# A new split of products between VectorE and GpSimd, and an input load whose last columns come in sixteen small pieces

## The chip, the core and the metric

The kernel runs on one core of one Trainium2 chip. The metric is the device time of one execution in microseconds (us), shorter is better. A profile gives the span from the first to the last instruction, and beside it the time of the very execution that was profiled.

## What is computed

For each of 4096 rows of 256 float32 numbers, all products of two of its numbers, i and j with j not below i, in the order of the upper triangle:

```python
def _L0_rec_ref(inputs):          # inputs: (4096, 256) float32
    d = inputs.shape[1]
    dot = jnp.einsum('bi,bj->bij', inputs, inputs)
    iu, ju = jnp.triu_indices(d)
    return dot[:, iu, ju]         # (4096, 32896) float32
```

The input has 4.2 MB, the output 4096 x 32896 x 4 bytes, 539 MB.

## The kernel before, in words

**Tiles and stages.** Each of the 128 partitions holds 32 rows of the input, and the whole input stays in SBUF as the tile `xt` (8192 numbers per partition, 512 of them for each pair of rows). Work goes two input rows at a time (`REPEAT`). The 32896 output columns of such a pair are cut into three pieces (`PIECES`): piece 0 has columns 0 to 10943, piece 1 columns 10944 to 21887, piece 2 the last 11008. Sixteen pairs of three pieces make 48 pieces. A piece is computed into one of two places in SBUF (`places`, the tiles o0 and o1, `o` in the profile) and then stored by a DMA of SP's queue. While one place is being stored, the other is filled. A place may be filled again when the store from it has landed (the semaphores `free`).

**A row of products.** "Row" in the code is a run of output columns with the same i: the products of number i with the numbers from i upwards, up to 256 long for i = 0 and 1 long for i = 255. Piece 0 holds 47 such rows (256 down to 203 long), piece 1 63 rows (the first of them a rest of 7 columns, then 209 down to 18 of the last one), piece 2 148 rows (147 down to 1). `vector_ops` puts two neighbouring rows into one instruction of double length where it can; what juts out of the first of them is overwritten later, and `interleave` and `schedule` lay the instructions out so that an overwriting one waits only for work that is long done. One instruction covers both input rows, so its number of elements per partition is twice the columns: 128x2x512 is a pair of rows 256 long for two input rows.

**The engines.** VectorE (`vector`) multiplies with one operand from SBUF (`xv`, a copy of the current pair's input) and one from PSUM (`xp`, another copy). GpSimd (`gpsimd`) reads both operands from `xv`. In the first two pieces (`AHEAD`), ScalarE helps (`scalar`). From then on a loop runs: its body covers six pieces (`PASS`) and is run eight times on VectorE and GpSimd, each by its own branch; the last two pieces of a body belong to the next pass and stand in an `If`.

**What sets the order.** The order is written out by hand. In the loop `blocks` cuts the rows of a piece at index `k = share(block)`: before the change the first k rows (the long ones) are VectorE's and the rest GpSimd's. `share` takes the k at which the larger of two estimates is least, `vector_time` of the first part and `gpsimd_time` of the second plus `LATER`. GpSimd starts a piece when VectorE's first instruction of it is done (semaphore `go`); VectorE's last instruction of a piece waits for GpSimd's last (`g_done`). SP waits for `v_done` and issues the store.

**The loads.** SP issues all input loads at the start, ahead of the first store on the same queue: the first pair of rows (128x512, semaphore `loaded[0]`) and all others (128x7680, `loaded[1]`). VectorE and GpSimd wait for the second one before the loop only.

Of the kernel before, what the change touches and what calls it, by code (L numbers as in the profile page):

```python
# [12 lines left out]
P = 128  # L13
UNIT = 64
REPEAT = 2
# [7 lines left out]
AHEAD = 2  # L23


LATER = 1.0
FIRST = [3968]
DIRECT = 1
COPY = 700
# [7 lines left out]
def runs(d: int, lo: int, hi: int) -> list:  # L37


    found, at = [], 0  # L40
    for i in range(d):
        a, b = max(at, lo), min(at + d - i, hi)
        if a < b:
            found.append((i, i + a - at, a, b - a))
        at += d - i
    return found


def vector_ops(block: list) -> list:

    ops, k = [], 0
    while k < len(block):
        i, j, at, n = block[k]
        m = 2 if k + 2 < len(block) and i == j else 1
        ops.append((block[k], m))
        k += m
    return ops  # L60
# [32 lines left out]


def vector_time(block: list) -> float:
    return sum(68 + 1.046 * REPEAT * n * m for (*_, n), m in vector_ops(block))


def gpsimd_time(block: list) -> float:
    return sum(142 + 1.66 * REPEAT * n * m for (*_, n), m in vector_ops(block))  # L100
# [6 lines left out]
def split(block: list, alone: bool, busy: list) -> int:  # L107

    def ends(k: int) -> list:
        vector = sum(vector_time([run]) for run in block[k:]) if alone else vector_time(block[k:])  # L110
        return [busy[0] + scalar_time(block[:k]), busy[1] + vector]

    k = min(range(len(block) + 1), key=lambda k: max(ends(k)))
    busy[:] = ends(k)
    return k


def tail(block: list, budget: float) -> int:
    return next(k for k in range(len(block)) if gpsimd_time(block[k:]) <= budget * 1e3)


def share(block: list) -> int:
    return min(range(len(block)), key=lambda k: max(vector_time(block[:k]), gpsimd_time(block[k:]) + LATER * 1e3))


def window(ap: bass.AP, free: list) -> bass.AP:
# [4 lines left out]
def kernel(  # L131
# [15 lines left out]
    nc = tc.nc  # L147
    n, d = x.shape
    width = out.shape[1]
    each, groups = REPEAT * d, n // (P * REPEAT)  # L150
# [8 lines left out]
    x_in = x.rearrange("(p g) d -> p (g d)", p=P)  # L159
# [5 lines left out]
    xt = pool.tile([P, groups * each], F32, name="x")  # L165
# [5 lines left out]
    def semaphore(name: str):  # L171
        return ctx.enter_context(nc.semaphore(name))

    free = [semaphore(f"free{k}") for k in range(PLACES)]
    head, v_done, a_done, go = (semaphore(s) for s in ("head", "v_done", "a_done", "go"))
    loaded = [semaphore(f"loaded{k}") for k in range(2)]

    def take(engine, sem, value: int):
        engine.wait_ge(sem, value).then_inc(sem, -value)  # L179
# [7 lines left out]
    def blocks(p: int, ahead: bool):  # L187

        lo, hi = spans[p % PIECES]
        alone = ahead and p == 0  # L190
        cuts, busy = [lo, *(FIRST if alone else []), hi], [0, 0]
        for c, (a, b) in enumerate(zip(cuts, cuts[1:])):
            block = runs(d, a, b)
            if c == DIRECT:
                busy[1] += COPY
            if ahead:
                if p == HELPED:
                    block = block[: tail(block, HELP)]
                k = split(block, alone, busy)
                yield a - lo, b - lo, block[:k], block[k:], lo  # L200
            else:
                k = share(block)
                yield a - lo, b - lo, block[k:], block[:k], lo

# [9 lines left out]
    def vector(h, pieces: range, ahead: bool, done: int = 0, joined: int = 0) -> tuple:  # L216
        for p in pieces:
            place, copied = places[p % PLACES], None
            parts = blocks(p, ahead)
            if ahead and p == 0:  # L220
                for c, (_, _, _, block, lo) in enumerate(parts):
# [67 lines left out]
    def scalar(pieces: range):  # L289

        xa = xt[:, :each]
        for p in pieces:
            for _, _, block, _, lo in blocks(p, True):
                todo = [
                    nc.scalar.activation(  # L295
                        places[p][:, r, at - lo : at - lo + length],
                        xa[:, r * d + j : r * d + j + length],
                        AF.Copy,
                        scale=xa[:, r * d + i : r * d + i + 1],
                    )  # L300
                    for i, j, at, length in block
                    for r in range(REPEAT)
                ]
                if todo:
                    todo[-1].then_inc(a_done, 1)
                else:
                    nc.scalar.sem_inc(a_done, 1)

    def gpsimd(h, pieces: range, ahead: bool, done: int = 0, turns: int = 0) -> tuple:
# [6 lines left out]
        for p in [HELPED] if ahead else pieces:  # L316
            place = places[p % PLACES]
            block, lo = helped(p) if ahead else next((block, lo) for _, _, block, _, lo in blocks(p, False))
            turns += not ahead
            order = interleave(block)  # L320
            waits = schedule(order)
            counted = {*waits.values()}
            number = {k: done + 1 + c for c, k in enumerate(sorted(counted))}
            for k, ((i, j, at, length), m, _) in enumerate(order):
                at -= lo
                ins = nc.gpsimd.tensor_tensor(  # L326
                    place[:, :, at : at + m * length],
                    window(xv[:, j:], [[d, REPEAT], [1, m], [1, length]]),
                    window(xv[:, i:], [[d, REPEAT], [1, m], [0, length]]),
                    ALU.mult,  # L330
                )
                if k == 0 and not ahead:
                    ins._wait_ge(go, turns)
                elif k in waits:
                    ins._wait_ge(g_own, number[waits[k]])
                if k in counted:
                    ins.then_inc(g_own, 1)
            done += len(counted)
            ins.then_inc(g_done, 1)
        return done, turns  # L340

    def sync():
        done = ahead_done = 0
        for turn in range(passes * PASS):
            h, p = divmod(turn, PASS)
            ahead, place = turn < AHEAD, places[p % PLACES]
            parts = list(blocks(p, ahead))
            for lo, hi, *_, base in parts:
                done += 1
                if ahead:  # L350
                    ahead_done += 1
                    nc.sync.wait_ge(a_done, ahead_done)
                to = x_out[h, p // PIECES, :, :, base + lo : base + hi]
                store = nc.sync.dma_start(to, place[:, :, lo:hi])
                store._wait_ge(v_done, done)
                store.then_inc(free[p % PLACES] if len(parts) == 1 else head, 16)
        for sem, count in ((v_done, done), (a_done, ahead_done)):
            nc.sync.sem_inc(sem, -count)

    def settle(engine, counts: tuple):  # L360
        for sem, count in zip((v_own, g_done) if engine is nc.vector else (g_own, go), counts):
            if count:
                engine.sem_inc(sem, -count)  # L363

    def all_pieces(engine, pieces_of):
        settle(engine, pieces_of(0, range(AHEAD), True))
        for sem in loaded[1:]:
            engine.wait_ge(sem, 16)
        kind = engine.engine
        with nc.Fori(  # L370
            0,
            passes,
            engines=OrderedEngineSet([kind]),
            head_slot={kind: 0},
        ) as h:
            counts = pieces_of(h, range(AHEAD, PASS), False)
            with engine.If(h < passes - 1):
                nxt = nc.s_assert_within(h + 1, 0, passes - 1)
                settle(engine, pieces_of(nxt, range(AHEAD), False, *counts))
        if engine is nc.vector:  # L380
            nc.vector.wait_ge(v_own, counts[0]).then_inc(v_done, 1)
        settle(engine, counts)

    for (lo, hi), sem in zip(((0, each), (each, groups * each)), loaded):
        nc.sync.dma_start(xt[:, lo:hi], x_in[:, lo:hi]).then_inc(sem, 16)
    nc.vector.memset(edge, 0.0).then_inc(warm, 1)  # L386
    take(nc.scalar, warm, 1)
    nc.scalar.activation(edge[:, :1], edge[:, 1:2], AF.Copy, scale=edge[:, 2:3])  # L388
# [5 lines left out]
    for engine, pieces_of in ((nc.vector, vector), (nc.gpsimd, gpsimd)):  # L394
        all_pieces(engine, pieces_of)
    sync()
    for sem in loaded:
        take(nc.sync, sem, 16)
    for k in range(PLACES):
        take(nc.sync, free[k], 16 * uses)  # L400

# [26 lines left out]
```

## Time and profile before

| what | value |
|---|---|
| median of 3 runs | 1264.88 us (1264.6 to 1265.08) |
| the profiled execution's own time | 1265.03 us |
| its span | 1262.8 us |
| VectorE (DVE) busy | 821.9 us, 65% |
| GpSimd (POOL) busy | 751.5 us, 60% |
| ScalarE (ACT) busy | 27.1 us, 2% |
| DMA | 543.22 MB, mean 430 GB/s |

The profiled execution lies inside the range of the runs, 0.15 us above their median; 2.2 us of it lie outside the span. Busy shares are means over the span; the DMA rate is that of all 16 DMA engines of the core together.

### The profile page before, as it was taken

The page shows a single profiled execution, that of the slowest core. Times are in us where ns is not written, and L with a number is a line of the kernel's source. Part 1 is how long each engine was busy: PE and PEld are TensorE (multiplying, and loading weights), DVE is VectorE, ACT ScalarE, POOL GpSimd, SP SyncE. Part 2 cuts the span into 40 slices and gives each one's busy share as a digit, 9 for nine tenths or more (in the row PEclk, how much of TensorE's full clock was granted, in tenths as well). Part 3 has the DMA queues.
Part 4 walks back from the last instruction along what each step waited for, and adds up shares of the span by engine and source line. Part 5 has one row for each costly group of instructions (what it writes and reads, how often), then busy time and mean ns, then how long its engine had stood idle before and what let it go on. Part 6 is the DMA issues. An engine that isn't in the chain of part 4 may idle for free. (4 is left out here: it accounts for less than half of the span.)

```text
span 1262.8 us, 2727 instructions
## 1 busy us (share of the span) xinstructions
DVE 821.9 (65%) x1234; ACT 27.1 (2%) x72; POOL 751.5 (60%) x1131
## 2 busy tenths in 40 slices
DVE  7657766677566775766657666576656766567660
ACT  8000000000000000000000000000000000000000
POOL 5556755567556664666546665576645766467650
DMA  9999999999999999999999999999999999999997
GB/s 390 433 442 426 441 426 438 430 437 434 433 436 432 434 433 434 432 436 431 436 430 440 427 441 426 441 425 442 427 440 427 439 428 438 428 441 428 439 433 331
DMA packets 13623, 543.22 MB, mean 430 GB/s; under 512 B 816, under 2 KB 816, under 8 KB 944
## 3 DMA queue, kind: packets, MB, share of 16 engines
q1 hardware_dynamic: 13616, 543.17, 99.5%
q14 instruction: 7, 0.06, 0.0%
HBM read 4.19 MB, written 538.97 MB: 430 GB/s over the span
## 5 line engine op out<-in xcount | busy, mean ns | idle before, releaser
L267 DVE TENSOR_TENSOR o<-xv,xp 128x504 f32<-128x504 f32 (+59 forms) x1175 | 791.1, 745 | 402.1 <-DMA out_dram<-o 264.2
L326 POOL TENSOR_TENSOR o<-xv 128x64 f32<-128x64 f32 (+61 forms) x1125 | 750.7, 708 | 466.1 <-DVE o L267 465.8
L295 ACT ACTIVATE o<-x 128x256 f32<-128x256 f32 (+34 forms) x70 | 25.5, 457 | 1.0 <-DMA x<-in_r_inputs_dram 1.0
L246 DVE COPY xp<-x 128x512 f32 x15 | 10.3, 686 | 0.0
L228 DVE TENSOR_TENSOR o<-x,xp 128x454 f32<-128x454 f32 (+17 forms) x18 | 9.4, 599 | 0.0
L228 DVE TENSOR_TENSOR o<-x 128x498 f32<-128x498 f32 (+8 forms) x9 | 5.3, 658 | 2.7 <-DMA x<-in_r_inputs_dram 2.7
L244 DVE COPY xv<-x 128x512 f32 x15 | 6.4, 426 | 0.6
L312 POOL MEMSET xv<- 128x1 f32 x1 | 0.1, 98 | 10.1 <-POOLq L179 10.1
L388 ACT ACT_TABLE_LOAD x1 | 1.3, 1283 | 1.2 <-ACTq L179 1.2
L386 DVE MEMSET edge<- 128x32 f32 x1 | 0.1, 85 | 1.0 <-SPq L169 1.0
L223 DVE COPY xp<-x 128x512 f32<-128x512 f32 x1 | 0.7, 681 | 0.0
L313 POOL COPY xv<-x 128x512 f32<-128x512 f32 x1 | 0.6, 609 | 0.0
L388 ACT ACTIVATE edge<-edge 128x1 f32<-128x1 f32 x1 | 0.3, 294 | 0.0
L415 POOL MEMSET const-float32-0.0<- 128x1 f32 x1 | 0.1, 98 | 0.2 <-issue 0.2
L415 POOL MEMSET const-bfloat16-1.0<- 128x1 bf16 x1 | 0.1, 101 | 0.0
L415 POOL MEMSET const-uint8-127<- 128x1 uint8 x1 | 0.1, 101 | 0.0
L415 POOL MEMSET const-float32-1.0<- 128x1 f32 x1 | 0.1, 98 | 0.0
## 6 DMA issues: line engine op xcount, KB each, us to landing
out_dram<-o SPq DMA_DIRECT2D x31, 10944.0 KB, 35.1
out_dram<-o SPq DMA_DIRECT2D x16, 11008.0 KB, 32.9
out_dram<-o SPq DMA_DIRECT2D x1, 6976.0 KB, 21.4
out_dram<-o SPq DMA_DIRECT2D x1, 3968.0 KB, 13.9
x<-in_r_inputs_dram SPq DMA_DIRECT2D x1, 3840.0 KB, 12.4
x<-in_r_inputs_dram SPq DMA_DIRECT2D x1, 256.0 KB, 2.8
```

The source lines that it names most:

```text
L223: nc.vector.tensor_copy(xp, x_of(h, 0)).then_inc(v_own, 1)
L228: ins = nc.vector.tensor_tensor(place[:, :, at - lo : at - lo + length], window(x_of(h, 0)[:, j:], [[d, REPEAT], [1, 1], [1, length]]), wi ...
L244: ins = nc.vector.tensor_copy(xv[:, :each], x_of(h, p // PIECES))
L246: nc.vector.tensor_copy(xp, x_of(h, p // PIECES)).then_inc(v_own, 1)
L267: ins = nc.vector.tensor_tensor(place[:, :, at : at + m * length], window(xv[:, j:], [[d, REPEAT], [1, m], [1, length]]), window(xp[:, i:] ...
L295: nc.scalar.activation(places[p][:, r, at - lo : at - lo + length], xa[:, r * d + j : r * d + j + length], AF.Copy, scale=xa[:, r * d + i ...
L312: nc.gpsimd.memset(xv[:, each:], 0.0).then_inc(g_own, 1)
L313: nc.gpsimd.tensor_copy(xv[:, :each], x_of(0, 0)).then_inc(g_own, 1)
L326: ins = nc.gpsimd.tensor_tensor(place[:, :, at : at + m * length], window(xv[:, j:], [[d, REPEAT], [1, m], [1, length]]), window(xv[:, i:] ...
L386: nc.vector.memset(edge, 0.0).then_inc(warm, 1)
L388: nc.scalar.activation(edge[:, :1], edge[:, 1:2], AF.Copy, scale=edge[:, 2:3])
L415: nc = _bacc.Bacc("TRN2", target_bir_lowering=False, num_devices=1)
```

## The change

Two edits, independent of one another.

The split in the loop: GpSimd now takes the first rows of a piece, which are the longest, and VectorE all rows after them. `share` takes the smallest k for which the estimate of VectorE's remaining rows is at most `BUDGET`, 19.5 us, and the constants of that estimate are new. The first two pieces are unchanged.

The load of the input: the second load is 64 columns (256 bytes) narrower, and these last 64 columns come in 16 further loads of 1, 2, 3 and so on to 15 rows, and 8 rows, partition after partition, with a semaphore of their own, for which VectorE and GpSimd wait before the loop.

```diff
-LATER = 1.0
+LAST = [k * (k + 1) // 2 for k in range(16)]
+BUDGET = 19.5
...
 def vector_time(block: list) -> float:
-    return sum(68 + 1.046 * REPEAT * n * m for (*_, n), m in vector_ops(block))
+    return sum(122 + 0.979 * REPEAT * n * m for (*_, n), m in vector_ops(block))
...
 def share(block: list) -> int:
-    return min(range(len(block)), key=lambda k: max(vector_time(block[:k]), gpsimd_time(block[k:]) + LATER * 1e3))
+    return next(k for k in range(len(block)) if vector_time(block[k:]) <= BUDGET * 1e3)
...
                 k = share(block)
-                yield a - lo, b - lo, block[k:], block[:k], lo
+                yield a - lo, b - lo, block[:k], block[k:], lo
...
-        for sem in loaded[1:]:
-            engine.wait_ge(sem, 16)
+        engine.wait_ge(loaded[1], 16)
+        engine.wait_ge(loaded[2], 16 * len(LAST))
...
-    for (lo, hi), sem in zip(((0, each), (each, groups * each)), loaded):
-        nc.sync.dma_start(xt[:, lo:hi], x_in[:, lo:hi]).then_inc(sem, 16)
+    def load(rows: slice, lo: int, hi: int, sem):
+        nc.sync.dma_start(xt[rows, lo:hi], x_in[rows, lo:hi]).then_inc(sem, 16)
+
+    load(slice(0, P), 0, each, loaded[0])
+    load(slice(0, P), each, groups * each - UNIT, loaded[1])
+    for k, lo in enumerate(LAST):
+        load(slice(lo, LAST[k + 1] if k + 1 < len(LAST) else P), groups * each - UNIT, groups * each, loaded[2])
```

In the third item that `blocks` yields stand GpSimd's rows, in the fourth VectorE's. The columns and instructions of each piece in the loop, counted from the code:

| piece | VectorE before | VectorE after | GpSimd before | GpSimd after |
|---|---|---|---|---|
| 0 | 7018 columns, 17 instructions | 8676, 22 | 3926, 12 | 2268, 7 |
| 1 | 7074, 22 | 8298, 27 | 3870, 15 | 2646, 10 |
| 2 | 7605, 36 | 6328, 59 | 3403, 44 | 4680, 21 |
| sum | 21697, 75 | 23302, 108 | 11199, 71 | 9594, 38 |

All of GpSimd's (POOL's) instructions of piece 0 in the loop before; in each, 128 partitions, two input rows, and the columns of one or two rows of products:

```order
L326 TENSOR_TENSOR o_60<-xv 128x2x454
L326 TENSOR_TENSOR o_60<-xv 128x2x448
L326 TENSOR_TENSOR o_60<-xv 128x2x442
L326 TENSOR_TENSOR o_60<-xv 128x2x432
L326 TENSOR_TENSOR o_60<-xv 128x2x426
L326 TENSOR_TENSOR o_60<-xv 128x2x225
L326 TENSOR_TENSOR o_60<-xv 128x2x222
L326 TENSOR_TENSOR o_60<-xv 128x2x438
L326 TENSOR_TENSOR o_60<-xv 128x2x214
L326 TENSOR_TENSOR o_60<-xv 128x2x211
L326 TENSOR_TENSOR o_60<-xv 128x2x217
L326 TENSOR_TENSOR o_60<-xv 128x2x203
```

The same place on GpSimd after:

```order
L327 TENSOR_TENSOR o_60<-xv 128x2x256
L327 TENSOR_TENSOR o_60<-xv 128x2x510
L327 TENSOR_TENSOR o_60<-xv 128x2x252
L327 TENSOR_TENSOR o_60<-xv 128x2x502
L327 TENSOR_TENSOR o_60<-xv 128x2x248
L327 TENSOR_TENSOR o_60<-xv 128x2x253
L327 TENSOR_TENSOR o_60<-xv 128x2x249
```

The rows 247 to 256 long have gone to GpSimd, all shorter ones to VectorE; seven instructions stand where twelve stood.

The start of SP's queue, before against after (from the first loads on; the rows go on with the loads of 8, 9 and up to 15 rows, one of 8 rows, and then the stores):

```order
+L386 DMA x<-in_r_inputs_dram 128x512
+L386 DMA x<-in_r_inputs_dram 128x7616
+L386 DMA x<-in_r_inputs_dram 1x64
+L386 DMA x<-in_r_inputs_dram 2x64
+L386 DMA x<-in_r_inputs_dram 3x64
+L386 DMA x<-in_r_inputs_dram 4x64
+L386 DMA x<-in_r_inputs_dram 5x64
+L386 DMA x<-in_r_inputs_dram 6x64
+L386 DMA x<-in_r_inputs_dram 7x64
```

Sixteen DMAs of SP now stand between the second load and the first store, where there were none.

More of the change, by code (lines that the diff above doesn't have):

```diff
@@ L175 @@
     head, v_done, a_done, go = (semaphore(s) for s in ("head", "v_done", "a_done", "go"))
-    loaded = [semaphore(f"loaded{k}") for k in range(2)]
+    loaded = [semaphore(f"loaded{k}") for k in range(3)]
     def take(engine, sem, value: int):
@@ L396 @@
     sync()
-    for sem in loaded:
-        take(nc.sync, sem, 16)
+    for sem, count in zip(loaded, (1, 1, len(LAST))):
+        take(nc.sync, sem, 16 * count)
     for k in range(PLACES):
```

## The prediction

> **What bounds the kernel now.** I read the page's head, queues and issues first, then the rate of the DMA by stretches, then the waits, then one pass of three pieces in the timeline. The page:
>
> ```profile
> span 1262.8 us, 2727 instructions
> ...
> q1 hardware_dynamic: 13616, 543.17, 99.5%
> q14 instruction: 7, 0.06, 0.0%
> ...
> out_dram<-o SPq DMA_DIRECT2D x31, 10944.0 KB, 35.1
> out_dram<-o SPq DMA_DIRECT2D x16, 11008.0 KB, 32.9
> ...
> x<-in_r_inputs_dram SPq DMA_DIRECT2D x1, 3840.0 KB, 12.4
> x<-in_r_inputs_dram SPq DMA_DIRECT2D x1, 256.0 KB, 2.8
> ```
>
> The 16 DMA engines are busy 99.5% of the span with SP's queue. By stretches (after the counts come the clock, the share of the 16 DMA engines, GB/s):
>
> ```profile
> 41.50:1248.00 1206.50, 797.03 (x1191) 0.00 (x0) 734.24 (x1109) 1.00 1.00 434
> ...
> 1249.00:1255.40 6.40, 0.00 (x0) 0.00 (x0) 0.00 (x0) 1.00 0.95 413
> 1255.40:1256.10 0.70, 0.00 (x0) 0.00 (x0) 0.00 (x0) 1.00 0.15 63
> 1256.10:1257.90 1.80, 0.00 (x0) 0.00 (x0) 0.00 (x0) 1.00 0.11 49
> 1257.90:1261.20 3.30, 0.00 (x0) 0.00 (x0) 0.00 (x0) 1.00 0.06 27
> 1261.20:1262.80 1.60, 0.00 (x0) 0.00 (x0) 0.00 (x0) 1.00 0.00 0
> ```
>
> In the loop nothing is left: 434 GB/s at a share of 1.00, 27.1 GB/s per engine. A store of 10944 KB (11.21 MB) takes 25.8 us. The end is what can still move. From 1256.1 on only one or two of the 16 engines work (0.11 x 16 = 1.8), from 1257.9 to 1261.2 exactly one, at its full 27 GB/s. All engines get the same bytes, so one DMA engine has fallen 5.1 us (1261.2 less 1256.1) behind fourteen others over 49 stores, a second one 1.8 us; the end waits for the first. Call it the late engine.
>
> The compute engines, in the waits:
>
> ```profile
> POOL o L326 <- DVE o L267: 465.8, 46, 14.1
> DVE o L267 <- DMA out_dram<-o: 264.2, 31, 9.5
> DVE o L267 <- DVEq L179: 109.3, 14, 9.9
> DVE o L267 <- POOL o L326: 11.9, 15, 0.8
> ```
>
> VectorE waits 264.2 + 109.3 = 373.5 us in 45 pieces, 8.3 us each, for a store that must land first (L179 is the same wait, taken in VectorE's queue); GpSimd waits behind VectorE. Neither sets the end.
>
> **The split, as compute time.** One pass (pieces 2, 0, 1, then 2 again) in the timeline (start, duration, engine, idle before):
>
> ```profile
> 118.75 18.67 DVE L267 TENSOR_TENSOR o<-xv,xp 128x260 f32<-128x260 f32 x36 [9.39 <-DMA out_dram<-o]
> 119.25 17.77 POOL L326 TENSOR_TENSOR o<-xv 128x328 f32<-128x328 f32 x44 [10.93 <-DVE o L267]
> ...
> 144.69 15.41 DVE L267 TENSOR_TENSOR o<-xv,xp 128x1024 f32<-128x1024 f32 x16 [6.21 <-DVEq L179]
> 145.99 14.87 POOL L326 TENSOR_TENSOR o<-xv 128x908 f32<-128x908 f32 x12 [8.96 <-DVE o L267]
> 160.89 0.64 DVE L267 TENSOR_TENSOR o<-xv,xp 128x466 f32<-128x466 f32 x1 [0.79 <-POOL o L326]
> 171.44 16.40 DVE L267 TENSOR_TENSOR o<-xv,xp 128x14 f32<-128x14 f32 x22 [9.91 <-DVEq L179]
> 171.69 15.12 POOL L326 TENSOR_TENSOR o<-xv 128x688 f32<-128x688 f32 x15 [10.84 <-DVE o L267]
> 197.10 13.28 DVE L267 TENSOR_TENSOR o<-xv,xp 128x260 f32<-128x260 f32 x24 [9.26 <-DMA out_dram<-o]
> ```
>
> Single products, by form (mean ns last):
>
> ```profile
> L326 POOL TENSOR_TENSOR o<-xv 128x908 f32<-128x908 f32 x12 | 20.4, 1698 | 108.9 <-DVE o L267 108.9
> ...
> L267 DVE TENSOR_TENSOR o<-xv,xp 128x1024 f32<-128x1024 f32 x12 | 14.7, 1221 | 75.8 <-DVEq L179 38.1 <-DMA out_dram<-o 37.7
> ...
> L326 POOL TENSOR_TENSOR o<-xv 128x320 f32<-128x320 f32 x12 | 8.6, 717 | 0.0
> ...
> L267 DVE TENSOR_TENSOR o<-xv,xp 128x512 f32<-128x512 f32 x12 | 8.1, 677 | 0.0
> ```
>
> VectorE's element costs (1221 - 677)/512 = 1.06 ns, GpSimd's (1698 - 717)/588 = 1.67 ns. Elements are twice the columns in the table of the change. Piece 0: 7018 columns are 14036 elements, 14.9 us; VectorE's 15.41 + 0.64 = 16.05 us leave 1.14 us for 17 products, 0.07 us each. Piece 2 gives 0.07 too, piece 1 0.06. GpSimd: 17.77 us less 6806 x 1.67 ns leaves 6.4 us for 44 products, 0.146 us each. After:
>
> - piece 0: VectorE 17352 x 1.0625 ns + 22 x 0.067 us = 19.9 us (was 16.05, and 0.79 of waiting for GpSimd); GpSimd 4536 x 1.668 ns + 7 x 0.146 us = 8.6 us (was 14.87).
> - piece 1: VectorE 16596 x 1.0625 ns + 27 x 0.062 us = 19.3 us (was 16.40); GpSimd 10.3 us (was 15.12).
> - piece 2: VectorE 12656 x 1.0625 ns + 59 x 0.07 us = 17.6 us; GpSimd 9360 x 1.668 ns + 21 x 0.146 us = 18.7 us, begun 0.5 us later, so that VectorE's last product waits for it: 19.4 us in all (was 18.67).
>
> So stores are issued at most 3.1 us later (piece 0: 19.9 against 16.84). What hides this: a store must start before the one ahead has left the queue. A place's store ends, 1.6 us later it counts as landed (the last row of stretches has 1.6 us without a byte), the piece is computed, and about 1 us after its issue the transfer can start. The store between takes 25.8 us, so a piece may take 23.2 us before the late engine runs dry: 3.3 us to spare at 19.9. The other engines are up to 5.1 us ahead and will run dry late in the run; they wait for the late one anyhow. Compute costs 0. The price from the forms alone, with no overlap of neighbouring products ((677 - 512 x 1.0625) = 133 ns each), would be 21.4 us for piece 0, still inside.
>
> **The split, as seen by the late engine.** No view names what holds this engine up. In the single packets behind the views, which no view groups, its packets are stretched mostly while compute engines run many short products; the other engines' are not. The price is bounded by who gets the blame for 5.1 us. A pass has 75 VectorE and 71 GpSimd products before, 108 and 38 after, 146 both times. All GpSimd's: 5.1 x (38/71 - 1) = -2.4 us. All VectorE's: 5.1 x (108/75 - 1) = +2.2 us. By the count of both, or by neither: 0. I take 85% GpSimd, since the stretched packets cluster in piece 2, where GpSimd has 44 products and VectorE 36, more strongly than the sum of both would have it: -0.85 x 2.4 + 0.15 x 2.2 = -1.7 us. No gain can exceed 3.3 us, since the second engine ends at 1257.9.
>
> The Trainium skill speaks against any effect: its page "SBUF — State Buffer", section "Who interferes with whom", says that a DMA never contends with a compute engine, apart from descriptors that GpSimd writes (here SP issues all). By that rule the split is worth 0 and the sum is the time of before; no run here shows yet which holds.
>
> **The loads.** SP's queue:
>
> ```profile
> L385 SPq DMA_DIRECT2D x<-in_r_inputs_dram x2: 390/403/416, 1.0 to 1.4; - x2
> ...
> DMA to landing us min/median/max: 2.8/7.6/12.4
> ...
> 0.96 0.86 SPq L385 DMA_DIRECT2D x<-in_r_inputs_dram  x2
> 9.58 0.40 SPq L354 DMA_DIRECT2D out_dram<-o  x1
> ...
> 2.00:12.80 10.80, 8.94 (x16) 9.77 (x26) 2.01 (x4) 1.00 1.01 388
> ```
>
> The last row is a stretch again: the first load is issued at 0.96 us and all engines are busy from 2.0 us on, which is the 1 us from issue to start used above.
>
> Sixteen issues more take 16 x 0.403 = 6.4 us: SP is done at 1.82 + 6.4 = 8.3 us, 1.3 us before the first store is issued at 9.58, which waits for products. And the engines have the second load to move until 1.4 + 12.4 = 13.8 us, so a store issued 2 or 3 us late would still lose nothing. If an issue of a short load took over 0.48 us, SP would be late, and from 0.6 us on the queue would run dry.
>
> The bytes are the same. What 16 loads cost the DMA engines before the first store has no row. Lower bound: a gain of 0.1 us, for an engine that gets none of the 128 short rows (2 KB less at 27 GB/s). Upper bound: one after the other, each with the 2.8 us of the first load, 45 us. The nearest row is that of the stores: 35.1 us from issue to landing for 25.8 us of transfer, at a share of 1.00, so the queue works through a later DMA without waiting for the earlier one's landing. I take 0.1 us, and 0 for the end unless the late engine is one that gets many. An offset on any other engine costs nothing below 5.1 us.
>
> The waits for the new semaphore stand before the loop, behind the two first pieces, and so behind loads that the queue carries out before the first store. VectorE's 108 products of code instead of 75 in a pass, is not refetched as long as the loop stays resident: the page has 7 packets of instructions in the whole span, though the body ran eight times.
>
> **The sum.** 1264.88 - 1.7 + 0 = 1263.2 us. The profiled execution (span 1262.8, itself 1265.03, 2.2 us outside the span) lies 0.15 us over the median; the difference of -1.7 is set against the median.
>
> **Rivals.**
>
> - Nothing moves (1264.9). The late engine's stretches go by the number of all products, or have nothing to do with them; this is also the page's rule. For: compute is hidden, the count stays 146. Against: the clustering in piece 2.
> - More is gained (1261.7): GpSimd's products are all of it and the second engine becomes the end, -2.4 to -3.3 us.
> - VectorE's products are the cause: +2.2 us, 1267.1. Against: piece 2 has just twice VectorE's products of piece 0, but almost four times GpSimd's.
> - Slower, by the loads: the short loads run one after the other on one engine, each for its own latency. It decides from 5.1/16 = 0.32 us per load on; at 2.8 us each, less 5.1 us of lead, about +40 us, 1305. Against: the stores' row above.
> - VectorE becomes the bound: from 23.2 us per piece on, each us more costs half a us per piece, some 23 us in 46 pieces. Against: the forms' upper price of 21.4.
>
> **How the numbers follow.** About 0.2%, 2.5 us, is what a measurement of this kernel can tell from no change; faster means below 1262.4, slower above 1267.4. Forecast, around -1.7 (-1.0 to -2.6): 0.45, a quarter of it beyond -2.5. Nothing moves: 0.25. More is gained: 0.15. VectorE the cause: 0.05, a fifth of it beyond +2.5. The loads in series: 0.06. VectorE bound or loop code fetched anew: 0.04. Faster: 0.11 + 0.15 = 0.26, and 0.04 for what an offset of the engines against one another might bring that I can't price, 0.30. Slower: 0.01 + 0.06 + 0.04 = 0.11, of which I keep 0.10. Same: 0.60. The range reaches from the ceiling of the gain, 1261.4, to 1265.8, just above the case in which nothing moves; the forecast's own is 1262.2 to 1263.9.
>
> **What would show it.** After: VectorE's pieces 0 and 1 at 19 to 20 us, its wait for stores down to 5 or 6 us per piece, its wait for GpSimd moved to piece 2; DMA share 1.00 in the loop; the single engine's tail at 27 GB/s shortened from 5.1 to about 3.4 us; the first store issued by 10 us. Wrong: the tail as long as before (nothing moves); a share below 1.00 in the loop (VectorE bound); a first store long after 10 us, or a gap behind the loads; more packets of instructions.

## The result and the profile after

The changed kernel takes 1266.91 us (median of 20 runs, 1266.47 to 1267.22) against 1264.93 us before in the same series: 1.0016 times as long, 95% interval 1.0009 to 1.0023. It is 2.0 us slower, where 1263.2 us and a range up to 1265.8 us were forecast. The profiled execution took 1266.93 us, its span is 1265.1 us (1262.8 before).

The page of the changed kernel: span, GpSimd's and VectorE's busy time, the queue, the large groups, and the DMA issues.

```profile
span 1265.1 us, 2746 instructions
...
DVE 899.3 (71%) x1752; ACT 27.1 (2%) x72; POOL 600.4 (47%) x613
...
q1 hardware_dynamic: 13872, 543.17, 99.5%
q14 instruction: 7, 0.06, 0.0%
...
L268 DVE TENSOR_TENSOR o<-xv,xp 128x156 f32<-128x156 f32 (+4 forms) x1693 | 868.5, 590 | 326.0 <-DMA out_dram<-o 193.5
L327 POOL TENSOR_TENSOR o<-xv 128x476 f32<-128x476 f32 (+20 forms) x607 | 599.5, 1027 | 620.0 <-DVE o L268 619.8
...
out_dram<-o SPq DMA_DIRECT2D x31, 10944.0 KB, 32.3
out_dram<-o SPq DMA_DIRECT2D x16, 11008.0 KB, 31.8
out_dram<-o SPq DMA_DIRECT2D x1, 6976.0 KB, 23.2
out_dram<-o SPq DMA_DIRECT2D x1, 3968.0 KB, 16.1
x<-in_r_inputs_dram SPq DMA_DIRECT2D x1, 3808.0 KB, 13.1
```

The DMA is as full as before (99.5%), and the code is not fetched anew (7 packets). The one row that has grown for the worse is the first store, the 3968 KB one: 16.1 us from issue to landing where it took 13.9. The stores of the loop land sooner after their issue (32.3 against 35.1), since they are issued later.

One pass in the timeline of the changed kernel (start, duration, engine, idle before):

```profile
121.36 17.16 DVE L268 TENSOR_TENSOR o<-xv,xp 128x448 f32<-128x448 f32 x58 [7.39 <-DMA out_dram<-o]
122.06 18.69 POOL L327 TENSOR_TENSOR o<-xv 128x260 f32<-128x260 f32 x21 [15.90 <-DVE o L268]
140.78 0.16 DVE L268 TENSOR_TENSOR o<-xv,xp 128x2 f32<-128x2 f32 x1 [2.27 <-POOL o L327]
...
147.27 19.61 DVE L268 TENSOR_TENSOR o<-xv,xp 128x988 f32<-128x988 f32 x22 [5.05 <-DVEq L180]
148.53 8.62 POOL L327 TENSOR_TENSOR o<-xv 128x512 f32<-128x512 f32 x7 [7.78 <-DVE o L268]
173.23 19.19 DVE L268 TENSOR_TENSOR o<-xv,xp 128x784 f32<-128x784 f32 x27 [6.34 <-DVEq L180]
```

Pieces of 19.6, 19.6 and 19.2 us, and VectorE still waits 5 us and more for a landed store ahead of each. The engines' rates by stretches, the load's end first, then the loop and the end (the last two columns are the share of the 16 DMA engines and GB/s; a packet counts whole in the stretch in which it starts, so a share can come out above 1):

```profile
13.20:16.20 3.00, 3.00 (x7) 3.00 (x9) 3.00 (x3) 1.00 1.06 342
...
41.50:1248.00 1206.50, 874.43 (x1709) 0.00 (x0) 583.09 (x591) 1.00 1.00 433
...
1254.90:1258.30 3.40, 0.00 (x0) 0.00 (x0) 0.00 (x0) 1.00 0.93 401
...
1258.60:1260.20 1.60, 0.00 (x0) 0.00 (x0) 0.00 (x0) 1.00 0.06 28
1260.20:1263.50 3.30, 0.00 (x0) 0.00 (x0) 0.00 (x0) 1.00 0.06 27
1263.50:1265.10 1.60, 0.00 (x0) 0.00 (x0) 0.00 (x0) 1.00 0.00 0
```

The tail of a single engine is still there, until 1263.5 now, 5.1 us after most others (1258.4). What is new stands in the first row. In the same 3 us before the change, the first store moved 434 GB/s:

```profile
13.20:16.20 3.00, 3.00 (x7) 3.00 (x9) 3.00 (x3) 1.00 1.01 434
```

At a share of 1.06 the engines count as busy and move a fifth less. The short loads themselves take little of that: in the single packets, which no view lists, each of the 128 rows of 256 bytes takes 18 ns, between 12.9 and 14.3 us, 2.3 us in all over 16 engines. It is the packets of the first store behind them that are stretched: those of 15872 bytes take 635 ns on average, up to 1791, where they took 592 before. And not on all engines. The packets bear no engine's name, but on one engine a packet starts where the one before it ends, and by that they can be followed, not always surely: an engine that carried 16 short rows loses 1.7 us in the first store, one with 12 about 1.3, one with 9 or 10 about 1.0, one with 5 or fewer nothing.

So the theory (A): the loads cost the time, by holding up the first store on those DMA engines that carry many short rows; the late engine is one of these, so its delay comes out at the end. The rivals: the split costs it (B), or each edit has a half (C).

### The profile page after: what moved, and what is told of

The parts are those of the page before. It is cut to its first block, busy times and chain, and to the rows that moved or that the text cites. A ratio compares the mean times of both kernels' runs of the same rounds, so it can differ in the third digit from the quotient of the medians.

```text
span 1265.1 us, 2746 instructions
## 1 busy us (share of the span) xinstructions
DVE 899.3 (71%) x1752; ACT 27.1 (2%) x72; POOL 600.4 (47%) x613
## 3 DMA queue, kind: packets, MB, share of 16 engines
q1 hardware_dynamic: 13872, 543.17, 99.5%
## 5 line engine op out<-in xcount | busy, mean ns | idle before, releaser
L268 DVE TENSOR_TENSOR o<-xv,xp 128x156 f32<-128x156 f32 (+4 forms) x1693 | 868.5, 590 | 326.0 <-DMA out_dram<-o 193.5
L327 POOL TENSOR_TENSOR o<-xv 128x476 f32<-128x476 f32 (+20 forms) x607 | 599.5, 1027 | 620.0 <-DVE o L268 619.8
L247 DVE COPY xp<-x 128x512 f32 x15 | 10.3, 686 | 0.0
## 6 DMA issues: line engine op xcount, KB each, us to landing
out_dram<-o SPq DMA_DIRECT2D x31, 10944.0 KB, 32.3
out_dram<-o SPq DMA_DIRECT2D x1, 3968.0 KB, 16.1
```

Source lines behind the costliest of these rows:

```text
L247: nc.vector.tensor_copy(xp, x_of(h, p // PIECES)).then_inc(v_own, 1)
L268: ins = nc.vector.tensor_tensor(place[:, :, at : at + m * length], window(xv[:, j:], [[d, REPEAT], [1, m], [1, length]]), window(xp[:, i:] ...
L327: ins = nc.gpsimd.tensor_tensor(place[:, :, at : at + m * length], window(xv[:, j:], [[d, REPEAT], [1, m], [1, length]]), window(xv[:, i:] ...
```

## Experiments: which edit, and which engine

All runs stand against the kernel before on the same chip.

**The split alone.** The changed kernel, with the loads of before.

```diff
-    load(slice(0, P), 0, each, loaded[0])
-    load(slice(0, P), each, groups * each - UNIT, loaded[1])
-    for k, lo in enumerate(LAST):
-        load(...)
+    for (lo, hi), sem in zip(((0, each), (each, groups * each)), loaded):
+        nc.sync.dma_start(xt[:, lo:hi], x_in[:, lo:hi]).then_inc(sem, 16)
```

> The changed kernel's split of products in the loop, with the loads of before (two loads, no short ones). Theory A, the loads cost the time: the split is worth nothing here, 1264.9 us, within 0.5 us, the first store lands 13.9 us after its issue as before, and the single engine's tail at the end is as long as before, about 5 us. Theory B, the split costs it (VectorE's 108 products a pass where it had 75, stores issued 3 us later): 1266.5 to 1267.2 us. Theory C, each edit has a half: about 1265.9 us.

Measured: 1265.18 us against 1265.10, ratio 1.0, interval 0.9991 to 1.001. Theory A. The tail is 4.6 us long (1256.8 to 1261.4). The stretches of this kernel have the changed kernel's products and the first store's full rate, nearly:

```profile
41.50:1248.00 1206.50, 874.72 (x1709) 0.00 (x0) 583.62 (x591) 1.00 1.00 433
...
13.20:16.20 3.00, 3.00 (x7) 3.00 (x9) 3.00 (x4) 1.00 0.98 418
```

**The loads alone.** The changed kernel, with `share` and `vector_time` of before.

```diff
-                yield a - lo, b - lo, block[:k], block[k:], lo
+                yield a - lo, b - lo, block[k:], block[:k], lo
```

> The split of before, with the changed kernel's loads (16 short ones of 1 to 15 and 8 rows). Theory A, the loads: 1266.6 to 1267.2 us, the first store lands about 16 us after its issue (13.9 before), and everything after it is shifted by 1.8 us. Theory B, the split: 1264.9 us, within 0.5 us. Theory C: about 1265.9 us.

Measured: 1267.13 us against 1265.10, ratio 1.0016 (1.0007 to 1.0025), +2.0 us. The whole loss is the loads'. Its first store:

```profile
13.20:16.20 3.00, 3.00 (x7) 3.00 (x9) 3.00 (x4) 1.00 1.04 334
...
out_dram<-o SPq DMA_DIRECT2D x1, 3968.0 KB, 16.6
```

**Whose delay counts.** Two kernels, both with the split of before, tell apart whether any delay of the first store costs time or only that of the late engine. In the changed kernel's trace the engine that ends last seems to be one that carried 12 short rows, as far as the packets can be followed. With loads of k rows on the first k engines that is the fifth: it gets a row of each of the 11 loads of 5 to 15 rows, and of the one of 8.

```diff
-LAST = [k * (k + 1) // 2 for k in range(16)]
+LAST = [*range(0, 64, 4), 64]        # 16 loads of 4 rows, one of 64
```

> The split of before; the last 256 bytes per row come in 16 short loads of 4 rows each and one of 64 rows. Theory A1: a short load holds up only the DMA engines that carry its rows, and the end feels it only where the late engine is among them; the late engine is the fifth, so loads of 4 rows, one row on each of four engines, miss it: 1264.9 us, 0.4 us more at most, though four engines are held up by 1.5 to 2 us and the first store lands 1.5 to 2 us later. Theory A2: whatever holds up some engine holds up the first store and with it the loop: 1266.5 to 1267.5 us, as with loads of 5 rows. The Trainium skill, page "DMA: Bandwidth & Descriptors", section "Why a DMA increments its semaphore by 16 and not by 1", says that a DMA of k rows issued by SP runs on the lowest-numbered k engines; that four rows always meet the same four engines rests on it.

```diff
-LAST = [k * (k + 1) // 2 for k in range(16)]
+LAST = [*range(0, 80, 5), 80]        # 16 loads of 5 rows, one of 48
```

> As the kernel with loads of 4 rows, but 16 short loads of 5 rows each and one of 48 rows, so that a fifth engine carries 16 short loads too. Theory A1 (only the late engine counts, and it is the fifth): 1266.8 to 1267.6 us, 2 us or more above the kernel with loads of 4 rows. If the late engine is another one: 1264.9 us, as with loads of 4 rows. Theory A2 (any engine counts): 1266.5 to 1267.5 us, equal to the kernel with loads of 4 rows.

Measured: with loads of 4 rows 1265.60 us, ratio 1.0004 (0.9995 to 1.0013); with loads of 5 rows 1268.07 us, ratio 1.0024 (1.0014 to 1.0033). One more row in each short load, on a fifth engine, costs 2.5 us. Yet the first store is held up alike in both (loads of 4 rows, then of 5):

```profile
out_dram<-o SPq DMA_DIRECT2D x1, 3968.0 KB, 17.0
...
13.20:16.20 3.00, 3.00 (x6) 3.00 (x9) 3.00 (x4) 1.00 0.96 349
```

```profile
out_dram<-o SPq DMA_DIRECT2D x1, 3968.0 KB, 17.0
...
13.20:16.20 3.00, 3.00 (x7) 3.00 (x9) 3.00 (x4) 1.00 0.99 344
```

The first store lands 17.0 us after its issue in both, later than in the changed kernel itself. In the single packets of the first store, four engines are held up by 1.8 to 1.9 us with loads of 4 rows, five by 1.8 to 2.1 us with loads of 5. Four engines held up by about 2 us disappear behind the late engine's 5 us; a fifth one does not, because it is the late one. That is theory A1, and it rules out A2. The Trainium skill, page "DMA: Bandwidth & Descriptors", section "Why a DMA increments its semaphore by 16 and not by 1", lets k rows run on the lowest-numbered k engines; the 2.5 us between loads of 4 and of 5 rows agree, and so do the four and the five stretched engines. The two times lie 0.3 and 0.5 us above the ranges of theory A1. The half us by which loads of 4 rows lie above the kernel before is inside that interval and stays open, and so does what it is in a short load that stretches the packets behind it.

**Where the short loads stand.** The same 16 short loads, ahead of the big load instead of behind it, with the split of before.

```diff
     load(slice(0, P), 0, each, loaded[0])
-    load(slice(0, P), each, groups * each - UNIT, loaded[1])
     for k, lo in enumerate(LAST):
         load(...)
+    load(slice(0, P), each, groups * each - UNIT, loaded[1])
```

> The split of before and the changed kernel's 16 short loads, issued ahead of the big load instead of behind it. Theory L: each short load holds its engine up by about 0.1 us wherever it stands, so the late engine still begins its stores 1.8 us later: 1266.9 to 1267.3 us. Theory S: the hold-up arises only where short loads stand directly ahead of the first store; ahead of a big load of ten times the packets' time it vanishes: 1265.1 us, within 0.4 us, and the first store lands about 14 us after its issue.

Measured: 1270.98 us against 1264.89, ratio 1.0048 (1.0034 to 1.0061): neither theory, and the first store lands 20.1 us after its issue, not 14. The expectation had left out SP's issue time. The 18 loads take SP 6.5 us to issue in either order, but here the big load is the last of them, and meanwhile the DMA has next to nothing to do:

```profile
0.96 6.47 SPq L386 DMA_DIRECT2D x<-in_r_inputs_dram  x18
...
2.00:8.00 6.00, 4.30 (x8) 5.10 (x13) 0.00 (x0) 1.00 0.17 48
8.00:13.00 5.00, 4.97 (x10) 5.00 (x15) 2.33 (x4) 1.00 1.05 390
```

In the single packets the big load ends at 19.4 us where it ended at 13.5 before: that is 5.9 of the 6.1 us. Those of the first store take 593 ns on average, as before the change, so the hold-up is gone. But the short loads were carried out one at a time as SP issued them, between 2.9 and 7.9 us, and the big load began at 8.0, when they were over. So this run shows that short loads which are long over hold up no store; it doesn't show what they do to a big load queued right behind them, and theory S is not tested as it was meant.

## Experiments: what makes the late engine late

The split moved 33 of GpSimd's 71 products per pass to VectorE, and the tail stayed as it was. Three kernels leave products out, with all stores kept.

```diff
 # few_pool: GpSimd keeps the last rows of a piece only
-                yield a - lo, b - lo, block[k:], block[:k], lo
+                yield a - lo, b - lo, block[-12 if p % PIECES == 2 else -4:], block[:k], lo
 # few_vector: VectorE keeps the first eight rows of a piece only
+                yield a - lo, b - lo, block[k:], block[:8], lo
 # few_both: both
+                yield a - lo, b - lo, block[-12 if p % PIECES == 2 else -4:], block[:8], lo
```

> Before, but GpSimd computes only the last few rows of each piece in the loop and leaves the others out (17 products a pass where it had 71; VectorE's 75 stay, 92 in all where 146 were). All stores stay. The question is what makes one DMA engine 5.1 us late at the end. Theory N, each product of VectorE or GpSimd costs it the same: the lag falls to 5.1 x 92/146 = 3.2 us, the time by 1.9 us, to about 1263.1. Theory G, only GpSimd's products cost it (what the prediction leaned to): the lag falls to 1.2 us and the second latest engine, 3.3 us ahead, becomes the end: about 1261.7. Theory V, only VectorE's: 1265.0. Theory 0, products have nothing to do with it: 1265.0.

> Before, but VectorE computes only the first eight rows of each piece in the loop and leaves the others out (21 products a pass where it had 75; GpSimd's 71 stay, 92 in all). Theory N: 1263.1 us, as with few products on GpSimd. Theory G: 1265.0. Theory V: the lag falls to 5.1 x 21/75 = 1.4 us, so about 1261.7 by the second latest engine. Theory 0: 1265.0.

> Both together: VectorE and GpSimd compute 38 products a pass instead of 146 and leave the rest out; all stores stay. Theories N, G and V: the late engine's lag falls to about 1.3 us, and the second latest engine, or one of the others, sets the end: 1261.5 to 1262. Theory 0: 1265.0 us with a lag of 5 us as before.

Measured, against 1265.00 us: fewer on GpSimd 1262.71 (0.9982, 0.9973 to 0.9992), fewer on VectorE 1262.72 (0.9982, 0.9973 to 0.9992), fewer on both 1260.85 (0.9968, 0.9955 to 0.998). The same stretch of the loop in the three, in this order:

```profile
41.50:1248.00 1206.50, 794.27 (x1191) 0.00 (x0) 109.92 (x264) 1.00 1.00 434
```

```profile
41.50:1248.00 1206.50, 190.92 (x352) 0.00 (x0) 734.86 (x1109) 1.00 1.00 434
```

```profile
41.50:1248.00 1206.50, 188.06 (x352) 0.00 (x0) 109.91 (x264) 1.00 1.00 434
...
1254.00:1256.00 2.00, 0.00 (x0) 0.00 (x0) 0.00 (x0) 1.00 0.46 198
1256.00:1258.70 2.70, 0.00 (x0) 0.00 (x0) 0.00 (x0) 1.00 0.00 0
```

845 products fewer on GpSimd (1109 - 264) are worth 2.29 us, 839 fewer on VectorE (1191 - 352) 2.28 us: 2.7 ns each, whichever the engine, where theory N had forecast 1.9 us. Both together are worth 4.15 us, near the sum; no packet starts after 1256.0, and in the single packets the last one ends at 1257.2, so of the tail little more than 1 us is left. That time is 0.7 us below the forecast, which had let the second latest engine set the end; in this run everything was over before that engine's 1257.9. The single packets say the same: from 41.5 to 1245 us, packets over 4 ns longer than their usual time lose 5.6 us in all before, 3.0 and 2.6 us in the first two kernels, 1.1 us in the third. Theory N holds; G, V and 0 fall. The busy time fell alike in the two (624 us on GpSimd, 606 on VectorE), so these runs alone don't tell number from busy time. The single packets of before and after do: summed over a piece, the stretching is 66, 93 and 217 ns in pieces 0, 1 and 2 before, with 29, 37 and 80 products whose busy time differs far less (30.9, 31.5 and 36.4 us), and in the first half of the passes after it is 68, 93 and about 210, with the same 29, 37 and 80 products otherwise shared out. (In the second half the sum of piece 2 rises to 380 ns and more; why is not shown.) What about a product reaches a DMA engine, and why mostly this one, stays open. One rival can't be ruled out here: every run on record has a span, so in every run each instruction was recorded while it ran, and a cost of the recording would also go by the number of products, on either engine. A run without a profile would tell.

**A version without the tail?** If the late engine is the fifth, it can be spared some bytes of the last store, by giving the last columns of it to DMAs that meet only the first four engines.

```diff
+RELIEF = 512
...
-                to = x_out[h, p // PIECES, :, :, base + lo : base + hi]
-                store = nc.sync.dma_start(to, place[:, :, lo:hi])
+                cut = RELIEF if turn == passes * PASS - 1 else 0
+                to = x_out[h, p // PIECES, :, :, base + lo : base + hi - cut]
+                store = nc.sync.dma_start(to, place[:, :, lo : hi - cut])
...
+                if turn == passes * PASS - 1:
+                    for rows in (slice(0, 124), slice(124, P)):
+                        to = x_out[h, p // PIECES, rows, :, base + hi - RELIEF : base + hi]
+                        nc.sync.dma_start(to, place[rows, :, hi - RELIEF : hi]).then_inc(free[p % PLACES], 16)
...
```

> Before, complete, but the last 512 columns of the last store go in two further stores of 124 and of 4 partitions. If the late engine is the fifth, it has 16 pieces of 2 KB less to store, 32 KB or 1.2 us at 27 GB/s, while the engines that take them are some 4 us ahead and get 3.6 us more: about 1263.9 us. If the late engine is one of the first four, it gets 3.6 us more: 1268.5. If the further stores cost a short transfer's hold-up of 0.1 us each only, nothing else changes. The Trainium skill, page "DMA: Bandwidth & Descriptors", section "Why a DMA increments its semaphore by 16 and not by 1", has k as the largest number up to 16 that divides the rows, on the lowest-numbered engines; that 124 and 4 rows both meet just the first four rests on it.

Measured: 1265.86 us against 1265.00, ratio 1.0007 (0.9998 to 1.0017): missed. The stretches of its end:

```profile
1257.00:1260.00 3.00, 0.00 (x0) 0.00 (x0) 0.00 (x0) 1.00 0.34 117
1260.00:1262.70 2.70, 0.00 (x0) 0.00 (x0) 0.00 (x0) 1.00 0.15 55
```

Now several engines work on, the last until 1262.6 (0.34 x 16 = 5.4, four of them and the late one): they were given too much. In the single packets the 64 pieces of 2 KB take 96 ns each on average (84 in the median), 6.1 us on each of the four. That is 4.9 us more than the 1.2 us saved, where I had counted 3.6, and I had taken all four to be 4 us ahead. In the kernel with loads of 4 rows, the single packets of those four engines end between 1258.3 and 1260.7 us, so they are not alike. Half the columns:

> As the relief of the last store, with 256 columns instead of 512. From the run with 512: the late engine is relieved by 0.6 us; the first four engines get 32 pieces of 1 KB less those they would have had, 64 in all, 3 us at most with their own cost, and the one of them that ends 1.8 us behind the others would end at about 1260.3 in the span, ahead of the late engine at 1260.6. So 0.5 us is gained, 1264.6 us. If the two stores cost over 0.7 us beyond their bytes, the first four set the end and nothing is gained, 1265.1.

Measured: 1264.33 us against 1264.89, ratio 0.9995 (0.9986 to 1.0004): 0.56 us less, the forecast size, but with no change still inside the interval. No version is shown here that beats the kernel before.

## Why the prediction was wrong

**Right: what bounds the kernel, and the compute side.** The DMA share stays 1.00 through the loop. VectorE's pieces 0 and 1 were put at 19.9 and 19.3 us and took 19.61 and 19.19; piece 2 at 19.4 in all, and took 19.58 (121.36 to 140.94). The wait for GpSimd moved to piece 2 (2.27 us there), GpSimd's 18.7, 8.6 and 10.3 us came out at 18.69, 8.62 and 10.32. VectorE waits (193.5 + 81.4)/45 = 6.1 us per piece for stores, where 5 or 6 were forecast. Waits of the changed kernel:

```profile
DVE o L268 <- DMA out_dram<-o: 193.5, 31, 7.4
DVE o L268 <- DVEq L180: 81.4, 14, 6.5
```

"The other engines ... will run dry late in the run" is what happened too: most of them now end within 0.2 us of one another (1258.1 to 1258.4), because they waited for the last store to be issued: SP issues it at 1231.2, and in the single packets these engines begin it between 1232.1 and 1232.4. The split alone shows the same and costs nothing (1265.18 against 1265.10 us).

**Right: the loads' issue.** SP takes 322 ns per load in the median, less than the 403 reckoned with, and the first store is issued at 9.59 us, as before (9.58).

**Two slips that decided nothing.** The late engine was 5.1 us behind thirteen others, not fourteen: the single packets of before end between 1255.4 and 1256.0 on thirteen engines, then at 1257.1, 1257.9 and 1261.2. And a gain of at most 3.3 us puts the lower end of the range at 1261.6, not 1261.4.

**Wrong: the split's -1.7 us.** It measured +0.08 us (interval of the ratio 0.9991 to 1.001). The step that failed is "I take 85% GpSimd, since the stretched packets cluster in piece 2". Piece 2 has the most of GpSimd's products and also the most of VectorE's, and I read the cluster as a difference between engines where it was one of numbers (the sums of a piece stand above). By the count of all products, a case the prediction had priced at 0, 146 are 146, and the runs with products left out put both engines at 2.7 ns per product. The Trainium skill's rule that a DMA never contends with a compute engine (page "SBUF — State Buffer", section "Who interferes with whom") gave the same 0 for the split, for another reason. The runs do not settle that rule: 1684 products fewer made the end 4.15 us earlier, which speaks against it unless the recording of the products is the cause.

**Wrong: the loads' 0.** They measured +2.0 us. The step is "I take 0.1 us, and 0 for the end unless the late engine is one that gets many". It is one that gets many: 12 of 16. And the hold-up is larger than 0.1 us: 1.7 to 2.1 us for an engine with 16 short loads and 1.3 us for one with 12, a little over 0.1 us for each short load, far below the 2.8 us of the upper bound but well above what the nearest row gave. Stores of 11 MB queue without a gap, and that row said nothing of DMAs of 256 bytes per engine. With the 12 rows themselves (18 ns each, 0.2 us) the late engine's 1.3 us explain 1.5 of the 2.0 us; the rest is as open as the half us of the loads of 4 rows. The condition was named and given no chance: that the late engine is among those with many short rows was not among the rivals at all, while "in series" was counted only from 0.32 us per load on, which holds for engines with 5 us to spare and for the late one not.

## What to carry to other kernels

When all DMA engines are full, the end belongs to the slowest of them, and a change is worth what it does to that one engine: find the tail (a share of one sixteenth, 0.06, at the rate of a single engine) before pricing anything, and ask of each DMA of few rows whether it meets that engine. Short DMAs right ahead of a long one on a queue are not free although their bytes nearly are: here 9 or more of them on an engine cost it about a tenth of a us each, 5 or fewer nothing. A cluster of stalls in the busiest stretch tells nothing of which engine causes them, as long as the engines' numbers rise together.

## What was not expected of the hardware

In these recorded runs each product on VectorE or GpSimd makes the end 2.7 ns later (2.29 us for 845 products, 2.28 for 839). The packets stretched in the loop before lose 5.6 us in 2300 products, hardly more than the late engine's 5.1 us, so little of it falls to the fifteen others. A short load's row of 256 bytes takes a DMA engine 18 ns, and the packets behind 16 of them lose 1.7 us, but nothing where the short loads are over before the big load begins (593 against 592 ns a packet).
